# A four-layer model on one core: dilated pieces spread over the expert turns, gathers of sequences 1 to 3 released earlier, and one-hots of the slot table moved from GpSimd to VectorE

## The chip, the cores and the metric

The kernel runs on one core of a Trainium2 chip. The metric is the device time of one execution in microseconds (us). The engines are named as in the profile: PE (TensorE, matrix products and transposes), DVE (VectorE), ACT (ScalarE), POOL (GpSimd, which also issues the indirect transfers) and SP (which issues the direct transfers).

## The reference

Four layers work on x of 4 sequences x 256 tokens x 256 features in f32. Every layer normalises x and adds an attention branch and a feed-forward branch of the same normalised input:

```python
xn = _layernorm(x)
x = x + attention(xn) + feed_forward(xn)     # four layers, each with its own two branches
```

- Layer 0: a gated linear scan, and a gated feed-forward network.
- Layer 1: dilated attention (segments of 64 tokens, 16 heads of 16 features, even heads see the even tokens of a segment, odd heads the odd ones), and 32 experts of which each token takes the 4 best:

```python
logits = x @ gate_w.T + gate_b
topk_logits, topk_idx = jax.lax.top_k(logits, K)            # E = 32, K = 4
topk_weight = softmax(topk_logits)
gate, up = ragged_dot(xt, w_gate, sizes) + b_gate, ragged_dot(xt, w_up, sizes) + b_up
gate, up = minimum(gate, 7), clip(up, -7, 7)
outs = ragged_dot((up + 1) * gate * sigmoid(1.702 * gate), w_down, sizes) + b_down
y = sum(outs * topk_weight)
```

- Layer 2: gated attention with 16 heads and two running states, and a block with latent attention and 8 experts (2 of 7 routed, 1 shared).
- Layer 3: causal attention with one head, and 8 experts of which each token takes 2.

## The kernel before, in words

x stays in the core's memory as 16 tiles of 128 tokens x 256 features. Four tiles are one sequence, called a block (NB = 4). `xn` holds the normalised tiles, `xnT` the same with features on the partitions. Each engine executes its own instructions in order. A scheduler places them in that order from the order in which the Python code issues them, from their dependencies, and from marks: under `self.tc.issue_after(self.mark)` instructions come behind the marked one, here the power that ends the last reciprocal root (`rsqrt`, L424: a scaling on POOL at L427 and a power on POOL at L429).

**Layer 1** (`layer1`, L1050) goes through these stages:

- *Places* (`places1`, L1245). The table `in_slot` says which token stands in which row of which expert's slots. For each of 16 tiles and each of a token's 4 experts m, DVE makes a one-hot `lane` (L1254) and DVE (m = 0) or POOL (m = 1 to 3) a one-hot `token` (L1256); PE multiplies the two (L1260) and adds them up. Both have a ring of 8 buffers. Every second tile one piece of the dilated units 0 and 1 is issued beside them.
- *Dilated units*. A unit is one block and one parity of heads: 8 units of 4 pieces each (`dilated`, L1400). The pieces issue (1) v and the queries q, by 8 steps on ACT (`scalar`) or one on DVE and one on POOL (L1421), (2) scores on PE (L1432) and their exponential on ACT (L1435), (3) pv on PE (L1444) and its copy on ACT, (4) transposes on PE (L1453) and the division and addition on DVE (L1455 to L1464).
- *Turns*. Rows gathered by POOL (L1315) are transposed by PE (L1327), multiplied by the expert's gate and up weights (L1343), combined on DVE (L1358), and multiplied by the down weights (L1364). There are 16 static turns (two blocks of rows each, one for each expert, weights loaded in groups), a number of pair turns (19 with these inputs) and of single turns (7), chosen at run time by a switch (`arms1`). Beside static turns `beside1` (L1174) issues the router's remaining products, one piece a turn; beside pair turns `beside2` (L1227) issues six pieces `eq` (four comparisons on DVE at L1238, each with a product on POOL at L1239, and sums) and the pieces of units 2 to 4, at 18 pieces over all pairs; beside the singles stands unit 5.
- *Collecting* (`collect1`, L1266). For one block POOL gathers 16 times 128 rows of the experts' outputs (L1275), and DVE adds each to x with its weight (`accumulate`, L532). The gathers land in the block's own `xn` and `xnT`, so there are 8 destinations and each is used twice. Block 0 is collected with units 6 and 7 beside it, then normalised (`layer_norm`: statistics at L438 and L439, the root on POOL at L427 and L429, `xn` on DVE at L457).

**Layer 2** (`layer2`, L1483) runs 32 gated units, unit u on block u % 4. A unit's supply (`gated_supply`) makes its projections (`pj`, L1659) from Wk, Ws and Wq, the clipped scores' exponential (eF, L1669 on DVE and L1670 on ACT) and transposes (`turn`, L1690); the unit itself makes scores (`sc`, L1722), values (`pt`, L1737) and the rest; the drain adds its output. `run` interleaves the steps of unit u (m), of the supply of u + 1 (s) and of the drain of u - 1 (d) by an order string written out by hand, and beside them the latent chain of the second branch (its first steps: `rmsq` on ACT at L1976, the root `rms` on POOL, `a` on DVE at L1979). The supply of unit u needs its block normalised, and for blocks 1 to 3 `normed` (L1510) first collects that block:

```python
if b:
    with self.tc.issue_after(self.mark):
        for _ in self.collect1(b):
            pass
    self.layer_norm(b)
```

`latent_tables` (L1909) prepares constants of the latent chain on POOL and DVE, among them the memset of `va` (L1915, L1916).

Of the kernel before, what the change touches and what calls it, by code (L numbers as in the profile page):

```python
# [15 lines left out]
NB = 4  # L16
# [99 lines left out]
class Net:  # L116
# [419 lines left out]
    def layer0(self):  # L536
# [9 lines left out]
        with ExitStack() as ctx:  # L546
# [30 lines left out]
                self.load_group(g)  # L577
            self.moe2, self.moe3 = self.expert_rows("l2", 7, 2), self.expert_rows("l3", 8, 2)
            self.latent_ahead(early)
            self.clear1()  # L580
            c_b, d1_b = cols[:, 0:2], cols[:, 6:14]
            agg_b, _, _, _, _, d2_b, bc_b, gate_b, out_g, out_b = (rows[:, i : i + 1, :] for i in range(10))
# [467 lines left out]
    def layer1(self):  # L1050
        nc, a, moe, r1 = self.nc, self.a, self.moe1, self.r1
        with ExitStack() as ctx:
# [17 lines left out]
            nc.scalar.mul(e.rearrange("p (i j) s n -> p i (j s n)", j=4), zeros(4), 0.0)  # L1070

            units = [(b, p) for b in range(NB) for p in range(2)]
            dilated = lambda u: self.dilated(*units[u], e, v, wa, pd, scalar=u < 2)
            early = [dilated(u) for u in range(2)]
            turns = iter([early[0]] * 3 + [early[1]] * 3)
            for _ in self.places1(wk, po):
# [29 lines left out]
            for pairs in self.arms1(0, [1 + 2 * i for i in range(PAIRS // 2 + 1)]):  # L1106
                line = Line(self)
                at = lambda n: 2 * n if n < STATIC // 2 + pairs else None
                pieces = self.beside1(bd, wa, ptr, pd)
                for n in range(STATIC // 2):  # L1110
                    line.turn(
                        dict(t=2 * n, n=n, parts=[static(2 * n), static(2 * n + 1)], done=static_done), at(n + 2)
                    )
                    if n in (8, 10):
                        self.fetch1(singles_at + n - 8, held[n // 2 - 4])
                    next(pieces, None)
                for _ in pieces:
                    pass

                def pair_done(j):  # L1120
                    if 2 <= j < pairs - 8:
                        self.load_expert(8 + (j - 2) % 8, j + 8)

                pieces = self.beside2([dilated(u) for u in (2, 3, 4)], wa)
                credit = 0.0
                for j in range(pairs):
                    line.turn(dict(t=STATIC + 2 * j, n=j, parts=pair(j), done=pair_done), at(STATIC // 2 + j + 2))
                    credit += 18 / pairs
                    while credit >= 0.999:
                        credit -= 1  # L1130
                        next(pieces, None)
                line.end(pieces)
            for singles in self.arms1(1, list(range(17))):
                line = Line(self)

                def single_done(k):
                    for j in (2 * k + 8, 2 * k + 9):
                        if j < 2 * singles:
                            self.load_expert((2 + j) % 8, 32 + j)

                for j in (6, 7):
                    if j < 2 * singles:
                        self.load_expert((2 + j) % 8, 32 + j)
                pieces = dilated(5)
                for k in range(singles):
                    line.turn(
                        dict(t=singles_at + 2 * k, n=k, parts=[single(2 * k), single(2 * k + 1)], done=single_done),
                        singles_at + 2 * k + 4 if k + 2 < singles else None,
                    )
                    next(pieces, None)  # L1150
                line.end(pieces)
            self.latent_loads()
            pieces = (piece for u in (6, 7) for piece in dilated(u))
            for n, _ in enumerate(self.collect1(0)):
                if n % 2:
                    next(pieces, None)
            for _ in pieces:
                pass
            self.layer_norm(0)
        self.routing.close()  # L1160
        self.stats = self.small
        self.ordered.close()
# [8 lines left out]
        for i in self.tc.Switch(index, len(counts)):  # L1171
            yield counts[i]

    def beside1(self, bd, wa, ptr, pd):  # L1174


        nc, r1 = self.nc, self.r1
# [46 lines left out]
                products(b)  # L1224
                yield

    def beside2(self, chains, wa):  # L1227

        nc, r1 = self.nc, self.r1
        slot, s8, w = r1["slot"], r1["s8"], r1["w"]  # L1230
        eqs = []
        for m in range(6):
            if m > 1:
                nc.vector.tensor_reduce(self.share1[:, :, m - 2], eqs[m - 2], AX.X, ALU.add)
            if m < 4:
                eq = wa.tile([P, 4, P], F32, tag="pvs", name="eq").rearrange("p a b -> p (a b)")
                eqs.append(eq.rearrange("p (i e) -> p i e", e=32))
                nc.vector.tensor_tensor(eqs[m], slot, s8[:, :, m : m + 1].to_broadcast([P, NTILE, 32]), ALU.is_equal)  # L1238
                nc.gpsimd.tensor_tensor(eqs[m], eqs[m], w, ALU.mult)  # L1239
            yield  # L1240
        for chain in chains:
            for _ in chain:
                yield

    def places1(self, wk, pool):  # L1245

# [4 lines left out]
        for i in range(NTILE):  # L1251
            for m in range(4):
                lane = wk.tile([P, P], F16, tag="lane", name="lane", bufs=8)
                nc.vector.tensor_scalar(lane, self.lane16, inside[:, i, m : m + 1], None, ALU.is_equal)  # L1254
                token = wk.tile([P, blocks], F16, tag="token", name="token", bufs=8)
                (nc.gpsimd if m else nc.vector).tensor_scalar(  # L1256
                    token, self.starts16[:, :blocks], first[:, i, m : m + 1], self.less[:, i : i + 1], ALU.is_equal,
                    ALU.mult,
                )
# [223 lines left out]
    def layer2(self):  # L1483
# [8 lines left out]
        with ExitStack() as ctx:  # L1492
# [8 lines left out]
            def supplied(u):  # L1501
# [5 lines left out]
                units[u] = {"b": b, "w": weights[pair]}  # L1507
                return self.gated_supply(units[u])

            def normed(b):  # L1510
                if b:
                    with self.tc.issue_after(self.mark):
                        for _ in self.collect1(b):
                            pass
                    self.layer_norm(b)
                yield
                self.to_features(
                    gp["ps"], self.xn[:, 4 * b : 4 * b + 4, :], self.xnT[:, :, b * T : (b + 1) * T], tag="ps"
                )
# [389 lines left out]
    def latent_tables(self):  # L1909
        nc, lp = self.nc, self.lp  # L1910
        rotk, rotq = lp["rot"]
        _, rk, up, _, _, _, shift_row = lp["w_"]
        sign = lp["sign"]
        for t in (self.w2, self.top2, lp["mt"], lp["va"]):
            nc.gpsimd.memset(t, 0.0)  # L1915
        nc.gpsimd.memset(lp["va"][:, :, :, 16:17], 1.0)  # L1916
        nc.gpsimd.memset(sign, 1.0)
        for j, lo in enumerate(lp["lows"]):

# [5 lines left out]
                out=lo, in_=lo, compare_op=ALU.is_ge, fill=1.0, base=32 * j + 31, pattern=[[0, 1]], channel_multiplier=-1  # L1925
            )
            nc.gpsimd.tensor_tensor(sign, sign, lo, ALU.mult)

        cols = lambda t: t.rearrange("p (h r) -> p h r", r=32)
        for k in range(KD):  # L1930
# [584 lines left out]
```

## Time and profile before

| what | value |
|---|---|
| median of 3 runs (lowest to highest) | 2217.51 us (2215.41 to 2227.51) |
| the profiled execution's own time | 2226.35 us |
| its span, first to last instruction | 2224.6 us |
| mean granted clock of PE in it | 0.917 |
| busy: PE, DVE, ACT, POOL | 88%, 54%, 37%, 30% of the span |
| chain that ended last | PE 57%, DVE 9%, issue 6%, POOL 5%, DMA 3% |

The chain that ended last is followed back from the last instruction, at each step to what released it. Times of single instructions come from the one profiled execution; its zero is the start of the span. In a line of the timeline stand start, busy time, engine, line, operation, output and inputs, count, and in brackets the idle time before it with what ended it. Where the kernel is in it: the places run from 177 to 216 us, static turns from about 227 to 291, pair turns to 371, single turns from 376 to 407, block 0 is collected and normalised until 455, and layer 2 follows.

### The profile page before, as it was taken

The numbers are of one execution on the slowest core, as the hardware profiler recorded it, in microseconds if no ns is written. First come the engines' busy times: TensorE is split into PE (matmuls) and PEld (weight loads), VectorE is DVE, ScalarE is ACT, GpSimd is POOL, SyncE is SP. The second block draws the span as 40 slices with busy tenths as digits, with TensorE's granted clock in tenths as the row PEclk, the third lists the DMA queues.
The fourth block names the chain that finished last, engine by engine and source line by source line (L and its number), as shares of the span: only waits on it lengthen the run. The fifth ranks groups of instructions, "written<-read, shape, count | busy, mean of one in ns | idle before, by whom it ended". The sixth has DMA issues, their size and how long they took to land.

```text
span 2224.6 us, 35391 instructions
## 1 busy us (share of the span) xinstructions
PE 1967.7 (88%) x13015; PEld 1441.2 (65%) x13015; DVE 1192.5 (54%) x3422; ACT 825.1 (37%) x1661; POOL 667.0 (30%) x782
## 2 busy tenths in 40 slices
PE   5754988448999999999999999999999988899995
PEld 2422877335666776666766676656787866678895
DVE  5745565458565655554655656555655564522223
ACT  1243344222433433433433444333345533334321
POOL 6328564464112121121111121111444351022231
PEclk9955999768999999999999999998899999899998
DMA  8312885531000000000000000001433320168697
GB/s 287 131 38 66 256 261 148 165 100 43 5 13 6 8 10 6 8 10 6 6 13 6 8 11 5 27 11 41 135 120 113 98 81 1 42 229 266 214 329 242
DMA packets 149548, 198.19 MB, mean 89 GB/s; under 512 B 16885, under 2 KB 127576, under 8 KB 149208
## 3 DMA queue, kind: packets, MB, share of 16 engines
q1 hardware_dynamic: 135224, 156.40, 21.6%
q0 software_dynamic: 14112, 39.15, 6.0%
q8 instruction: 110, 1.80, 0.3%
q14 instruction: 102, 0.84, 0.1%
HBM read 154.21 MB, written 41.29 MB: 88 GB/s over the span
## 4 chain that ended last, share of the span: by engine, by line
PE 57%; DVE 9%; issue 6%; POOL 5%; DMA 3%; ACT 1%; another core or an unknown queue 1%; SPq 0%; POOLq 0%; DVEq 0%; ACTq 0%
PE pt L1737 8%; PE pj L1659 6%; PE o L1850 4%; PE g L2266 4%; PE kq L2081 3%; PE pov L1801 3%; PE sc L1722 3%; DVE junk L2056 2%; PE o L2279 2%; PE qk L2049 2%; PE pv L2097 2%; DMA r<-l_rows,in_slot 2%; PE st L1710 1%; PE turn L1690 1%; PE pov L1807 1%
## 5 line engine op out<-in xcount | busy, mean ns | idle before, releaser
L2056 DVE CUSTOM_DVE_ANT_0 junk<-qk,hide 128x512 f32<-128x512 f32 (+3 forms) x256 | 124.6, 487 | 41.9 <-PE qk L2049 23.9
L2089 POOL TENSOR_SCALAR_AFFINE_SELECT pr<-pr 128x512 f32<-128x512 f32 x64 | 40.3, 643 | 339.1 <-ACT pr L2086 339.1
L2266 PEld LDWEIGHTS g<-rT,we 128*128 128x128 f32 x1120 | 131.4, 193 | 5.4 <-ACT rT L376 3.0
L2266 PE MATMUL g<-rT,we 128*128 128x128 f32 x1120 | 132.3, 277 | 1.9 <-ACT rT L376 1.9
L343 POOL DMA_INDIRECT r<-l_rows,in_slot x73 | 71.2, 975 | 191.4 <-PE rt L374 105.8
L383 POOL DMA_INDIRECT l_outs<-y,to x73 | 72.5, 993 | 183.6 <-ACT y L382 148.9
L1737 PE MATMUL pt<-Wg,xnT 128*128 128x256 f32 x512 | 125.3, 397 | 2.1 <-DVE both L361 1.0
L1850 PE MATMUL o<-Wo,oT 128*128 128x256 f32 x512 | 121.7, 381 | 0.0
L1737 PE MATMUL pt<-Wv,xnT 128*128 128x256 f32 x512 | 120.1, 386 | 0.0
L1728 DVE TENSOR_TENSOR s<-sc,keep 128x512 f32<-128x512 f32 x128 | 82.5, 683 | 68.1 <-PE sc L1722 68.1
L1672 DVE RECIPROCAL rz<-rz 128x128 f32<-128x128 f32 x128 | 116.8, 933 | 0.4
L1737 PEld LDWEIGHTS pt<-Wg,xnT 128*128 128x128 f32 x512 | 97.9, 197 | 26.6 <-issue 8.5
L355 DVE TENSOR_TENSOR mine<-r,number 128x2 f32<-128x2 f32 x73 | 13.1, 180 | 174.8 <-DMA r<-l_rows,in_slot 174.7
L2086 ACT ACTIVATE pr<-kq 128x512 f32<-128x512 f32 (+1 forms) x192 | 86.2, 530 | 50.1 <-PE kq L2081 49.6
L1737 PEld LDWEIGHTS pt<-Wv,xnT 128*128 128x128 f32 x512 | 94.9, 191 | 15.0 <-issue 0.2
L1315 POOL DMA_INDIRECT r<-l_rows,in_slot x84 | 82.8, 986 | 72.2 <-PE rt L1327 30.5
L1850 PEld LDWEIGHTS o<-Wo,oT 128*128 128x128 f32 x512 | 96.0, 197 | 8.3 <-issue 0.5
L2081 PE MATMUL kq<-q,kT 32*128 32x128 f32 (+3 forms) x512 | 89.3, 497 | 7.4 <-DVE mx L2056 5.9
L1818 DVE TENSOR_TENSOR o<-pov,g 128x512 f32<-128x512 f32 x64 | 41.3, 686 | 77.2 <-ACT sq L1817 77.2
L1740 ACT COPY v<-pt 128x512 f32<-128x512 f32 x64 | 37.5, 586 | 120.4 <-PE pt L1737 119.3
L1823 POOL TENSOR_TENSOR rs<-ms,sm 128x8 f32<-128x8 f32 x32 | 6.5, 204 | 240.3 <-DVE ms L1821 240.2
L2033 POOL TENSOR_TENSOR q<-q 128x512 f32<-128x512 f32 x16 | 20.3, 1269 | 192.2 <-DVE q L2030 192.2
(561 smaller groups left out, 4664.6 us busy)
## 6 DMA issues: line engine op xcount, KB each, us to landing
we<-l_w SPq DMA_DIRECT2D x70, 512.0 KB
we<-l_wo SPq DMA_DIRECT2D x35, 512.0 KB
l_outs<-none SPq DMA_DIRECT2D x1, 11776.0 KB
l_outs<-y SPq DMA_DIRECT2D x42, 256.0 KB
we<-l_r_gate SPq DMA_DIRECT2D x38, 128.0 KB
we<-l_r_up SPq DMA_DIRECT2D x38, 128.0 KB
we<-l_r_down SPq DMA_DIRECT2D x38, 128.0 KB
l_rows<-xn SPq DMA_DIRECT2D x8, 544.0 KB
```

Source lines behind the costliest of these rows:

```text
L343: self.nc.gpsimd.indirect_dma_start(out=r[:, m, :], out_offset=None, in_=moe["rows"][:, :], in_offset=bass.IndirectOffsetOnAxis(ap=moe["in ...
L383: self.no_order(moe["name"] + " back", nc.gpsimd.indirect_dma_start(out=moe["outs"][:, :], out_offset=bass.IndirectOffsetOnAxis(ap=to, axi ...
L1315: nc.gpsimd.indirect_dma_start(out=r[:, i, :], out_offset=None, in_=moe["rows"][:, :], in_offset=bass.IndirectOffsetOnAxis(ap=moe["in_slot ...
L1659: nc.tensor.matmul(ps, w[n][:, k, :], self.xnT[:, k, t["b"] * T : (t["b"] + 1) * T], start=(k == 0), stop=(k == KD - 1))
L1672: inverse = lambda c: nc.vector.reciprocal(rz[:, c * P : (c + 1) * P], rz[:, c * P : (c + 1) * P])
L1728: nc.vector.tensor_tensor(s, ps[hh], keep4, ALU.mult)
L1737: nc.tensor.matmul(ps[:, i, :], self.xnT[:, k, s : s + P], w[n][:, k, :], start=(k == 0), stop=(k == KD - 1))
L1850: nc.tensor.matmul(ps[:, p, :], of_parity(oT[:, h, c * D : (c + 1) * D], p), wo[:, h, :], start=(h == 0), stop=(h == 1),)
L2056: nc.vector.tensor_tensor_reduce(out=junk[:, :m], in0=tiles[j][:, off : off + m], in1=self.hide[:, T - m :], op0=ALU.add, op1=ALU.max, sca ...
L2081: nc.tensor.matmul(tiles[j][:, BLOCK[i] - off : BLOCK[i] - off + T - i * P], kT[r, i * P : (i + 1) * P], qT[r, i * P :], start=True, stop= ...
L2086: nc.scalar.activation(pr[:, j, off : off + m], tiles[j][:, :m], AF.Exp, scale=0.25)
L2266: nc.tensor.matmul(pt[:, m, :], we[:, q, k * T + m * P : k * T + (m + 1) * P], rT[:, k, :], start=(k == 0), stop=(k == KD - 1),)
```

## The change

- In `places1` POOL makes only the token one-hots of m = 3; DVE makes m = 0 to 2.
- `beside2` is joined to `beside1`. The 35 pieces left (router, six eq, units 2 to 5) are issued over the static and the pair turns together, at 35 / (16 + pairs - 1) a turn. No dilated piece is left beside the singles.
- The queries of units 6 and 7 are made by ACT. Their pieces stand at fixed gathers of block 0's collection, unit 7's last piece behind block 0's norm.
- The mark that held the gathers of blocks 1 to 3 behind a norm is gone. The gathers are issued in steps of `run` (two a step in unit 0, alternately two and one in units 1 and 2), and these units have another order string. The supply of the next unit is built when its first step is due.
- The memsets and sign selections of the latent tables move to layer 0 (`latent_signs`); only the two memsets of `va` stay in `latent_tables`.

```diff
@@ layer 0
             self.latent_ahead(early)
+            self.latent_signs()
@@ layer1
-            dilated = lambda u: self.dilated(*units[u], e, v, wa, pd, scalar=u < 2)
+            dilated = lambda u: self.dilated(*units[u], e, v, wa, pd, scalar=u < 2 or u > 5)
...
-                pieces = self.beside1(bd, wa, ptr, pd)
+                pieces = self.beside1(bd, wa, ptr, pd, [dilated(u) for u in (2, 3, 4, 5)])
+                credit, rate = 0.0, 35 / (STATIC // 2 + pairs - 1)
                 for n in range(STATIC // 2):
...
-                    next(pieces, None)
-                for _ in pieces:
-                    pass
+                    credit += rate
+                    while credit >= 0.999:
+                        credit -= 1
+                        next(pieces, None)
...
-                pieces = self.beside2([dilated(u) for u in (2, 3, 4)], wa)
-                credit = 0.0
                 for j in range(pairs):
...
-                    credit += 18 / pairs
+                    credit += rate
...
-                pieces = dilated(5)
                 for k in range(singles):
...
-                    next(pieces, None)
-                line.end(pieces)
+                line.end(iter(()))
             self.latent_loads()
-            pieces = (piece for u in (6, 7) for piece in dilated(u))
+            last = [dilated(u) for u in (6, 7)]
+            next(last[0])
+            turns = {1: 0, 4: 0, 5: 1, 8: 1, 10: 0, 12: 1}
             for n, _ in enumerate(self.collect1(0)):
-                if n % 2:
-                    next(pieces, None)
-            for _ in pieces:
-                pass
+                if n in turns:
+                    next(last[turns[n]])
             self.layer_norm(0)
+            for chain in last:
+                for _ in chain:
+                    pass
@@ places1
-                (nc.gpsimd if m else nc.vector).tensor_scalar(
+                (nc.gpsimd if m == 3 else nc.vector).tensor_scalar(
@@ layer2
+            def supplies(u):
+                yield from supplied(u)
+
             def normed(b):
                 if b:
-                    with self.tc.issue_after(self.mark):
-                        for _ in self.collect1(b):
-                            pass
+                    for _ in collects[b]:
+                        pass
                     self.layer_norm(b)
...
-                supply = supplied(u + 1) if u + 1 < UNITS else iter(())
+                supply = supplies(u + 1) if u + 1 < UNITS else iter(())
+                gathered = collects.get(u + 1, iter(()))
...
-                for what in "mmmmsmsmmdmmsmsdmsd" if u + 1 < UNITS else "mmmmdmmdmmdmmm":
+                order = "mmmmsmsmmdmmsmsdmsd" if u + 1 < UNITS else "mmmmdmmdmmdmmm"
+                for n, what in enumerate("mmmmmmmdmmmsmsmdssds" if u < NB - 1 else order):
                     next(chains[what], None)
+                    for _ in range(2 - (u and n % 2)):
+                        next(gathered, None)
...
+            collects = {b: self.collect1(b) for b in range(1, NB)}
@@ latent_tables, its first lines now latent_signs
-        for t in (self.w2, self.top2, lp["mt"], lp["va"]):
+        for t in (self.w2, self.top2, lp["mt"]):
             nc.gpsimd.memset(t, 0.0)
-        nc.gpsimd.memset(lp["va"][:, :, :, 16:17], 1.0)
...
+    def latent_tables(self):
+        nc.gpsimd.memset(lp["va"], 0.0)
+        nc.gpsimd.memset(lp["va"][:, :, :, 16:17], 1.0)
```

More of the change, by code (lines that the diff above doesn't have):

```diff
@@ L1172, in arms1, with beside1 @@
             yield counts[i]
-    def beside1(self, bd, wa, ptr, pd):
+    def beside1(self, bd, wa, ptr, pd, chains):
         nc, r1 = self.nc, self.r1
@@ L1225, in beside1 @@
                 yield
-    def beside2(self, chains, wa):
-        nc, r1 = self.nc, self.r1
         slot, s8, w = r1["slot"], r1["s8"], r1["w"]
@@ L1241, in beside2 @@
         for chain in chains:
-            for _ in chain:
-                yield
+            yield from chain
     def places1(self, wk, pool):
@@ L1907, in latent_loads, with latent_signs @@
         self.load(ow, a["l2_o_w"].rearrange("(k p) n -> p k n", p=P))
-    def latent_tables(self):
+    def latent_signs(self):
         nc, lp = self.nc, self.lp
-        rotk, rotq = lp["rot"]
-        _, rk, up, _, _, _, shift_row = lp["w_"]
         sign = lp["sign"]
-        for t in (self.w2, self.top2, lp["mt"], lp["va"]):
+        for t in (self.w2, self.top2, lp["mt"]):
             nc.gpsimd.memset(t, 0.0)
-        nc.gpsimd.memset(lp["va"][:, :, :, 16:17], 1.0)
         nc.gpsimd.memset(sign, 1.0)
@@ L1927, in latent_tables @@
             nc.gpsimd.tensor_tensor(sign, sign, lo, ALU.mult)
+    def latent_tables(self):
+        nc, lp = self.nc, self.lp
+        rotk, rotq = lp["rot"]
+        _, rk, up, _, _, _, shift_row = lp["w_"]
+        sign = lp["sign"]
+        nc.gpsimd.memset(lp["va"], 0.0)
+        nc.gpsimd.memset(lp["va"][:, :, :, 16:17], 1.0)
         cols = lambda t: t.rearrange("p (h r) -> p h r", r=32)
```

## The prediction

> **What bounds the kernel now.** First the 40 slices of the page, to find where TensorE (PE) is short of work.
>
> ```profile
> PE   5754988448999999999999999999999988899995
> POOL 6328564464112121121111121111444351022231
> PEclk9955999768999999999999999998899999899998
> ```
>
> A slice is 55.6 us. From slice 10 (556 us) on PE stands at 8 or 9, so work there can only be cut, and the change cuts none. The holes lie before: slice 3 (167 to 222 us) and slices 7 to 9 (389 to 556), with POOL at 5 and 4, 4, 6. A microsecond gained there brings forward the start of the full stretch, and so the end. The chain that ended last agrees: PE 57%, DVE 9%, POOL 5%. Second, the table by stage (us, then busy time of PE, PEld, DVE, ACT, POOL, then clock, DMA share, GB/s):
>
> ```profile
> 170.00:216.00 46.00, 19.69 (x193) 11.83 (x194) 25.87 (x114) 17.01 (x33) 40.62 (x50) 0.54 0.22 70
> ...
> 411.00:455.00 44.00, 10.18 (x137) 7.40 (x137) 16.70 (x45) 6.88 (x15) 23.75 (x23) 0.51 0.35 110
> 455.00:500.00 45.00, 23.50 (x104) 14.92 (x105) 25.38 (x60) 10.67 (x31) 33.81 (x37) 0.65 0.40 120
> 500.00:545.00 45.00, 37.98 (x175) 21.49 (x171) 39.42 (x98) 7.66 (x14) 22.77 (x24) 0.81 0.19 56
> 545.00:700.00 155.00, 153.44 (x1057) 101.73 (x1056) 91.35 (x217) 63.13 (x113) 25.18 (x28) 0.98 0.02 7
> ```
>
> In 170 to 216 POOL is busy 40.62 of 46. Between 411 and 545 PE is idle 62 of 134 us; after 545 it is full. Third, POOL's and PE's timelines in that hole:
>
> ```profile
> 411.83 1.80 POOL L1915 MEMSET both<- 128x2048 f32 x1 [20.30 <-DMA l_outs<-y]
> ...
> 452.96 0.20 POOL L427 TENSOR_SCALAR rs<-mv 128x4 f32<-128x4 f32 x1 [13.78 <-DVE mv L439]
> 453.24 1.05 POOL L429 TENSOR_TENSOR rs<-rs,neghalf 128x4 f32<-128x4 f32 x1
> ...
> 475.35 1.04 POOL L429 TENSOR_TENSOR rms<-rms,neghalf 128x4 f32<-128x4 f32 x1
> ```
>
> ```profile
> 448.27 1.11 PE L1453 MATMUL pvt<-ident,pvs 128*128 128x128 f32 x4 [0.71 <-ACT pvs L1449]
> 454.79 2.08 PE L472 MATMUL tr<-ident,xn 128*128 128x128 f32 x8 [5.41 <-DVE xn L457]
> ...
> 488.76 2.08 PE L472 MATMUL tr<-ident,xn 128*128 128x128 f32 x8 [6.58 <-DVE xn L457]
> 490.77 2.08 PE L1722 MATMUL sc<-qT,kT 64*128 64x128 f32 x16
> ```
>
> Expert outputs are complete at 411.83; block 0 is normalised when unit 7's last piece is through (448.27), and gated unit 0's first scores (490.77) stand on PE behind the features of block 1, whose 16 gathers POOL only starts after block 0's norm.
>
> **Part 1, the places.** Each of 16 tiles needs 4 lanes and 4 tokens. Now POOL makes 48 tokens in one piece of 38.91 us (176.96 to 215.87), 0.81 each:
>
> ```profile
> L1256 POOL TENSOR_SCALAR token<-starts,first,less x48: 786/791/1094, 177.0 to 215.1; 128x126 f16<-128x126 f16 x48
> L1256 DVE TENSOR_SCALAR token<-starts,first,less x16: 299/348/449, 178.3 to 210.2; 128x126 f16<-128x126 f16 x16
> ```
>
> After, POOL makes 16 (16 x 0.81 = 13 us, no longer the limit) and DVE 48. DVE's steps in its timeline: four lanes take 0.81 us (190.20 to 191.01), a token 0.22 to 0.26. A tile is 0.81 + 3 x 0.24 = 1.53, 16 tiles 24.5: from 176.96 to 201.4. PE also carries six pieces of units 0 and 1 here, and its next one-hot product waits behind each: the ring of 8 lanes lets DVE run two tiles (3 us) ahead, while the wait for e on ACT is 1.28 (table) + 2.43 plus scores of 1.9 for unit 0 and 2.43 + 1.9 for unit 1. That leaves 2.6 + 1.4, and 1.3 for the last products and in_slot: 206.7 against 216.2, a gain of 9.5; I take **9.2**. Bounds: DVE tokens at a step of 0.31 add 3.4, so 6; no stall left, 13.
> The rows above were taken with POOL busy beside DVE throughout, so they hold what the two do to each other. The Trainium skill, "GPSIMD Engine Reference", section 1 (Specifications), speaks against the move: GpSimd's SBUF interface is shared with VectorE, and two-port modes contend. By it, DVE one-hots at their slowest (0.45) would make the 48 tokens 10 us longer and the gain nothing; the steps of 0.22 to 0.26 beside a busy POOL do not show that, and I go by them.
> Everything from the first gather (216.82) moves with it: DMA share is 0.43 in 216 to 240 and 0.98 in 240 to 270 with PE busy 29.87 of 30, so loads do not yet hold PE there.
>
> **Part 2, dilated units 2 to 5.** 35 pieces at 35/34 a turn: 16 now fall into the 16 static turns and 19 into the 19 pair turns. Before it was 13, the end, and 18. Unit 5's scores (1.08), pv (1.08) and pvt (0.60) go from the singles to the pairs, where PE is full (40.03 of 41.00 in 330 to 371): +2.8. The singles lose 1.81 + 1.08 + 0.60 = 3.5, partly idle anyway. The eq products on POOL (1.31 each, behind DVE's, with gathers queued behind; PE waits of 0.52, 1.58, 1.09 and 2.12 in 292 to 330) start in static turns instead: the same waits earlier. I take **0**, bounds -4 and +4.
>
> **Part 3, units 6 and 7.** q goes from POOL (2 x 1.9) and DVE (2 x 1.22) to 8 ACT steps of 0.42 a unit. From 411.17: v 0.5, q 3.4, scores 1.9, e 2.4, pv 1.9; unit 7 behind it ends about 437, 11 us before 448.27. It leaves the path.
>
> **Part 4, gathers and norm.** Block 1 to 3's gathers lose the mark that held them behind block 0's norm. In the changed program's POOL order that norm's rs stands behind 39 gathers and two memsets, its power behind 40; before, behind 16. A gather costs 0.96 + 0.30 issue = 1.26. 411.83 + 39 x 1.26 + 2.0 = 463.0; 0.3, one gather, power 1.05: xn starts at 465.6 against 454.32. This is 11.3 **late**: DVE's xn, PE's features and three products wait for it, and PE is idle from 437 to 466.
> What is won comes after. Then 8 gathers (10.1), rms and rs 0.5, one gather 1.26, power 1.05: 478.6 (475.35 + 1.04 before). DVE: three a at 0.38, eF 0.7: 480.4. ACT's exponential 0.7, then rmsq of block 1 and qT (0.6 each): 482.9. Unit 0's scores now stand ahead of block 1's features on PE: **482.8 against 490.77**. The last gather is issued about 505 (528.55 before), so no later unit waits longer for its block than before, and I carry **8.0** through to 545. Bounds: 0 if a chain of unit 0 that was hidden sets the pace, 16 if unit 1's gathers now cost PE nothing. The order strings of units 0 to 2 only permute work in a stretch that waits; SP's latent loads now precede Wk, Ws, Wq, all needed only at 468, 50 us after issue. latent_signs adds about 1 us of POOL work before the start's rs; PE then waits 3.33 us for weights (at 23.66): 0. A latent memset of 1.8 moves behind 22 gathers, counted above.
>
> **Sum.** 9.2 + 0 + 8.0 = 17.2. The profiled execution (2226.35 = span 2224.6 + 1.75 around it) becomes 2209.2, its span 2207.4. It lies 8.8 above the median of 2217.51; the stages moved are far shorter than that ratio could touch, so I take the same 17.2 from the median: **2200.3**.
>
> **Rivals.** (a) *Given back*: the norm that is 11 us late. At a pitch of 1.43 a gather, 49 gathers delay unit 0 by 49 x 0.17 = 8 and part 4 brings nothing; with places at 6 to 9 the time is 2208 to 2212. For it: blocks 1 to 3 took 1.56 a gather before, norms and waits included (454.48 to 529.5). Against: pitch 1.26 wherever POOL did not wait. (b) *Slower*: the same queue at a worse pitch. Eight transfers are in flight, and each gather waits for the one eight before and, in a block's second half, for DVE's accumulation, which stands in order among others. From a pitch of 1.83 unit 0 is 28 - 8 = 20 late, places give back 9, and the time is 2228.6; at 2.0 it is 2237. For it: DVE accumulates of block 0 now stand behind block 1's. Against: landing took about 3 us (454.48 to 457.51), far below eight pitches. (c) *More*: places 13, part 4 16: 2188. (d) *Spread does nothing*: part 4's gathers are not beside gated units at all, since 39 of 64 precede the norm; true of the order, and already in my sum.
>
> **Numbers.** No change is within 0.5%, 11 us: 2206 to 2229. My forecast (2194 to 2206) 0.44, (c) 0.16: faster 0.60. (a) and smaller gains 0.28. (b) 0.12. Range 2186 to 2228: above it lies (b), below it all parts at their best.
>
> **What would show it.** in_slot at about 207 with POOL's tokens no longer one solid block; outputs complete near 402; POOL's rs of block 0 after 39 gathers, 51 us after that; unit 0's scores 71 us after it, not 79; unit 1's (546.24 before) at 529. Wrong if DVE's tokens step by over 0.45, if gathers step by over 1.43, or if PE's idle time between the last expert and the full stretch, now 62 us, is not some 8 smaller.

## The result, and the profile after

The change makes the kernel slightly slower, by less than 1%. Beside runs of the kernel before (median 2221.35 us) the changed kernel has a median of 2235.62 us (2224.51 to 2250.46); the ratio is 1.0073, 95% interval 1.0052 to 1.0095. The forecast was 2200.3. The profiled execution took 2224.51 us, its span is 2222.8 us, and it is the fastest of the changed kernel's runs.

The slices of the changed kernel's page, to be laid beside those of before:

```profile
PE   5755988158999999999999999999999988899995
POOL 6324573553112112121111121111444352022231
PEclk9955999568999999999999999999899999899998
```

Slice 3 of POOL has gone from 8 to 4: the places no longer fill it. The hole of PE has moved forward with layer 1 (slice 7 holds 1, slice 8 holds 5), but it isn't narrower, and slice 9 is still 8. The table by stage says the same in microseconds (length, then busy time of PE, PEld, DVE, ACT, POOL, then clock, DMA share, GB/s):

```profile
170.00:216.00 46.00, 21.55 (x212) 14.14 (x213) 34.42 (x165) 17.05 (x33) 23.59 (x27) 0.57 0.30 92
...
411.00:455.00 44.00, 6.26 (x72) 4.01 (x72) 14.43 (x41) 7.24 (x16) 27.83 (x29) 0.50 0.30 87
455.00:500.00 45.00, 28.86 (x144) 19.36 (x145) 25.20 (x67) 14.16 (x37) 24.23 (x28) 0.73 0.32 96
500.00:545.00 45.00, 36.37 (x154) 19.66 (x153) 35.43 (x88) 7.31 (x13) 18.12 (x18) 0.81 0.09 24
545.00:700.00 155.00, 149.51 (x1002) 96.28 (x1002) 85.91 (x196) 60.18 (x109) 22.41 (x24) 0.98 0.02 7
```

Layer 1 ends 14.9 us earlier (ACT's copy of the last down product is through at 394.3 against 409.2). Between 411 and 545 PE is still idle 62.5 of 134 us, as before, although this stretch now begins 15 us later in the work; and from 545 to 700, which was full, PE is idle 5.5 us. What layer 1 won is lost in the first gated units.

The places themselves, the token rows of the changed kernel:

```profile
L1254 DVE TENSOR_SCALAR token<-starts,first,less x48: 300/308/437, 177.9 to 203.8; 128x126 f16<-128x126 f16 x48
L1254 POOL TENSOR_SCALAR token<-starts,first,less x16: 802/860/893, 176.7 to 202.6; 128x126 f16<-128x126 f16 x16
```

POOL's 16 tokens no longer fill the stretch (16 x 0.86 = 13.8 of 26 us), the chain of lanes and tokens on DVE sets the pace, and `in_slot` is done at 204.9 against 216.5.

### The profile page after: what moved, and what is told of

It is laid out like the page before. It is cut to its first block, busy times and chain, and to the rows that moved or that the text cites. A ratio compares the mean times of both kernels' runs of the same rounds, so it can differ in the third digit from the quotient of the medians.

```text
span 2222.8 us, 35354 instructions
## 1 busy us (share of the span) xinstructions
PE 1959.6 (88%) x13015; PEld 1432.5 (64%) x13015; DVE 1188.3 (53%) x3448; ACT 833.8 (38%) x1681; POOL 641.3 (29%) x748
## 4 chain that ended last, share of the span: by engine, by line
PE 55%; issue 8%; DVE 8%; POOL 6%; DMA 3%; ACT 2%; another core or an unknown queue 1%; SPq 0%; POOLq 0%; DVEq 0%; ACTq 0%
PE pt L1742 8%; PE pj L1664 6%; PE o L1855 4%; PE kq L2091 3%; PE sc L1727 3%; PE pov L1806 2%; PE g L2276 2%; PE qk L2059 2%; DVE junk L2066 2%; PE pv L2107 2%; DMA r<-l_rows,in_slot 2%; POOL l_outs L383 1%; PE turn L1695 1%; PE st L1715 1%
## 5 line engine op out<-in xcount | busy, mean ns | idle before, releaser
L2066 DVE CUSTOM_DVE_ANT_0 junk<-qk,hide 128x512 f32<-128x512 f32 (+3 forms) x256 | 124.1, 485 | 42.8 <-PE qk L2059 24.5
L355 DVE TENSOR_TENSOR mine<-r,number 128x2 f32<-128x2 f32 x73 | 12.8, 175 | 182.0 <-DMA r<-l_rows,in_slot 175.7
L2091 PE MATMUL kq<-q,kT 32*128 32x128 f32 (+3 forms) x512 | 90.3, 485 | 9.7 <-DVE mx L2066 8.1
L2091 PEld LDWEIGHTS kq<-q,kT 32*128 32x128 f32 x512 | 40.0, 189 | 55.8 <-DVE mx L2066 34.4
```

The lines of the kernel that those rows point to most:

```text
L2066: nc.vector.tensor_tensor_reduce(out=junk[:, :m], in0=tiles[j][:, off : off + m], in1=self.hide[:, T - m :], op0=ALU.add, op1=ALU.max, sca ...
L2091: nc.tensor.matmul(tiles[j][:, BLOCK[i] - off : BLOCK[i] - off + T - i * P], kT[r, i * P : (i + 1) * P], qT[r, i * P :], start=True, stop= ...
```

## The experiments

Lines of the changed kernel are a few lower than before's (L1727 is `sc`, L1664 `pj`, L2091 `kq`, L1451 `pvt`). Four chips served the experiments, A to D in the order below, each with its own runs of the kernel before; ratios are against those. One number sorts the profiles better than the span, because it has no part of the 1,550 us that follow: the time from T0, POOL's first instruction after its wait for the experts' outputs, to the scores of units 0 and 4. In the kernel before, v1_places and v3_layer2 that instruction is the memset of the latent tables, 2.2 us ahead of block 0's first gather; in the others it is the gather. The kernel before was profiled on the first chip only.

| kernel | chip | T0 | to unit 0 | to unit 4 | ratio (95%) |
|---|---|---|---|---|---|
| before | first | 411.8 | 78.9 | 255.5 | 1 |
| after | first | 397.7 | 81.4 | 273.1 | 1.0073 (1.0052 to 1.0095) |
| v1_places | A | 397.2 | 79.1 | 254.9 | 0.9938 (0.9918 to 0.9958) |
| v2_layer1 | A | 398.6 | 73.8 | 251.0 | 0.9930 (0.9906 to 0.9955) |
| v3_layer2 | A | 408.7 | 87.1 | 275.8 | 1.0129 (1.0108 to 1.0151) |
| v4_after | A | 397.5 | 81.4 | 272.8 | 1.0051 (1.0026 to 1.0076) |
| v5_order | B | 401.5 | 63.5 | 266.9 | 1.0017 (0.9998 to 1.0036) |
| v6_hoist | B | 399.8 | 72.2 | 247.4 | 0.9944 (0.9926 to 0.9962) |
| v8_spread | B | 402.3 | 72.1 | 247.3 | 0.9957 (0.9938 to 0.9976) |
| v10_hold | B | 398.9 | 65.8 | 243.0 | 0.9931 (0.9910 to 0.9953) |
| v7_drain | C | 396.0 | 71.9 | 246.8 | 0.9957 (0.9940 to 0.9973) |
| v9_half | C | 400.6 | 72.0 | 256.5 | 0.9990 (0.9972 to 1.0009) |
| v12_both | C | 397.5 | 45.3 | 239.4 | 0.9958 (0.9943 to 0.9974) |
| v13_after | C | 401.5 | 71.9 | 260.5 | 1.0011 (0.9991 to 1.0031) |
| v14_marks | D | 399.6 | 43.8 | 234.0 | 0.9889 (0.9871 to 0.9906) |
| v15_hold | D | 397.7 | 65.5 | 243.4 | 0.9937 (0.9911 to 0.9963) |
| v16_hoist | D | 397.6 | 72.3 | 245.2 | 0.9949 (0.9932 to 0.9967) |
| v17_after | D | 396.6 | 72.3 | 260.9 | 1.0015 (0.9995 to 1.0035) |

### Which half loses: chip A

**v1_places** is the kernel before with one line of the change:

```diff
-                (nc.gpsimd if m else nc.vector).tensor_scalar(
+                (nc.gpsimd if m == 3 else nc.vector).tensor_scalar(
```

> The kernel before with the places' edit alone (POOL makes the token one-hots of m = 3 only). Theory A (the layer-1 part gains, the layer-2 part gives it back): in_slot 11 to 12 us earlier, as in the changed kernel (204.9 against 216.5), and all of it at the end: 9 to 12 us under before. Theory B (what is gained ahead of layer 2 is swallowed there whatever layer 2 does): in_slot as early, but the total within 4 us of before.

2208.85 us against 2224.2. **v2_layer1** is the changed kernel with layer 2's steps as before:

```diff
-                    for _ in collects[b]:
-                        pass
+                    with self.tc.issue_after(self.mark):
+                        for _ in self.collect1(b):
+                            pass
...
-                for n, what in enumerate("mmmmmmmdmmmsmsmdssds" if u < NB - 1 else order):
+                for what in "mmmmsmsmmdmmsmsdmsd" if u + 1 < UNITS else "mmmmdmmdmmdmmm":
```

> The changed kernel with layer 2's supplies, mark and order string as before: places, spread, units 6 and 7 and latent_signs are kept. Theory A: block 0's norm stands behind 16 gathers again; its xn starts 12 to 16 us earlier than before's 454.3, and the total is 12 to 16 us under before, some 2206. Theory B: 2221 to 2236, like before or the changed kernel.

2210.21 us. **v3_layer2** is the reverse: the kernel before with those steps of layer 2 as the change has them.

> The kernel before with layer 2's part of the change alone (no mark, gathers in the steps of run, new order string). Theory A: unit 0's scores no earlier than before, unit 4's 15 us later, and the total 15 to 25 us over before, 2236 to 2246. Theory B: within 5 us of before. A third reading C, that the two parts only hurt together (units 6 and 7 among hoisted gathers): also within 5 us of before, but then the run with layer 1 alone is faster.

2255.37 us. **v4_after** is the changed kernel again.

> The changed kernel once more, for a second profile. Its 19 executions lay between 2224.5 and 2250.5, the profiled one at the lowest. Theory A: some 14 us over before on this chip. If the profile falls at 2240 or above, its mean clock is 0.915 instead of 0.925 and the extra half-clock time tells where the spread arises; ACT's wait of 32.8 us before the copy of unit 6's pv shows whether it comes back.

2232.14 us. The directions are theory A's, the sizes are not: v1_places gains 15 us (9 to 12 were expected), v3_layer2 loses 31 (15 to 25), v4_after 8 (14). So the places alone bring 0.6%, the rest of layer 1's part adds nothing that these intervals can see, and layer 2's part loses 1.2 to 1.3% on this chip whichever layer 1 it stands behind: the forecast had it at 8 us of gain.

### The hoist and the order string: chip B

**v5_order** is v2_layer1 with the new order string alone, so the marks that hold the gathers are back:

```diff
-                for what in "mmmmsmsmmdmmsmsdmsd" if u + 1 < UNITS else "mmmmdmmdmmdmmm":
+                for what in "mmmmmmmdmmmsmsmdssds" if u < NB - 1 else order:
```

> The run with layer 1's part alone, plus the new order string of units 0 to 2 (eager supplies and the mark stay). Theory A1 (of the 22 us that layer 2's part costs, the order string costs most: units 0 to 3 took 60.3 + 51.6 + 45.4 us against 57.6 + 45.3 + 39.7, 14.7 us more): total 10 to 15 us over the layer-1 run, near 2222; unit 0's scores as early (472) and unit 4's 10 to 15 us later (660 to 665). Theory A2 (the gathers between cost it): within 3 us of the layer-1 run.

2218.57 us against 2215.46. **v6_hoist** is the changed kernel with the old string alone; its gathers stay released:

```diff
-                for n, what in enumerate("mmmmmmmdmmmsmsmdssds" if u < NB - 1 else order):
+                for n, what in enumerate(order):
```

> The changed kernel with the old order string in units 0 to 2; gathers without the mark and issued in the steps of run as changed. A1: xn of block 0 still at 460, 25 us later than with the mark, unit 0's scores near 479, but units 0 to 2 at the pace of before: total 10 to 15 us under the changed kernel, near 2222. A2: within 3 us of the changed kernel, 2235.

2201.22 us. The string carries the loss: it takes away with the old gathers what layer 1 won (0.993 for v2_layer1 and v10_hold, 1.0017 for v5_order), and leaving it out gives it back with the new ones. With the old gathers it costs more than expected: 20.8 us between v10_hold, described below, and v5_order, which also differ in v10's copy, against 10 to 15 expected. **v8_spread** is v1_places with units 2 to 5 spread over the turns:

> The kernel with the places' edit alone, plus the spread of units 2 to 5 over static and pair turns. Prediction's part 2: 0 (-4 to +4) against the places alone. Rival: the six eq pieces now stall the last static turns (PE idle 6.3 us in 270 to 292 in the changed kernel, none before), 3 to 6 us over the places alone.

2206.45 us, 0.9957 against 0.9938 for v1_places on another chip: so 0.19%, 4 us, slower, with intervals that overlap. That fits the forecast of nothing, and it fits the rival of 3 to 6 us as well. On one chip, v2_layer1, which has the spread too, stands level with v1_places. **v10_hold** is v2_layer1 with a copy on POOL that reads unit 6's products, so that the later gathers of block 0 wait for them:

```diff
-            turns = {1: 0, 4: 0, 5: 1, 8: 1, 10: 0, 12: 1}
+            turns = {1: 0, 7: 0, 8: 1, 10: 0, 11: 1, 13: 1}
...
+        if b == NB - 1 and p == 0:
+            nc.gpsimd.tensor_copy(self.small.tile([P, 4], F32, tag="wsum", name="hold"), pvs[:, 0, :4])
```

> The run with layer 1's part alone, with one copy of 4 columns on POOL that reads unit 6's pv copy and so holds gathers 9 to 16 of block 0 back until it is made; unit 6's pv stands at gather 7. Theory P (PE's last product of a piece is reported late while POOL issues gathers: 406.5 by the record, 421.4 by ACT, POOL's sixteenth gather ending at 418.3): with POOL stopped after 8 gathers the copy starts within 2 us of pv's end, near 408 to 411, the norm of block 0 comes up to 8 us earlier, and the total is 3 to 8 us under the layer-1 run. Rival Q (the delay is PE's or ACT's own, fetching instructions after the switch): the copy starts at 421 again, gathers 9 to 16 wait for it, and the total is 10 us over.

2197.79 us, level with v2_layer1's ratio. It decides nothing between theories P and Q: on this chip the copy follows the recorded end of the product within 0.1 us without the hold as well (v5_order, v6_hoist).

### What in the string: chip C

The new string differs twice (steps counted from 0): the drain of the unit before comes at step 7 instead of 9, and the first steps of the next unit's supply (s) come at 11 instead of 4. **v7_drain** keeps the supply where it was and takes the early drain, **v9_half** puts the first two steps of the supply early and the last three late:

```diff
-                for n, what in enumerate("mmmmmmmdmmmsmsmdssds" if u < NB - 1 else order):
+                for n, what in enumerate("mmmmsmsdmmmmsmsmdmsd" if u < NB - 1 else order):
```

```diff
-                for n, what in enumerate("mmmmmmmdmmmsmsmdssds" if u < NB - 1 else order):
+                for n, what in enumerate("mmmmsmsdmmmmmmmdssds" if u < NB - 1 else order):
```

> The changed kernel with the old order string in units 0 to 2, except that the first drain step stands at place 7 instead of 9, as in the new one (mmmmsmsdmmmmsmsmdmsd). Theory S (the new string costs because the next unit's supply, five steps of projections, exponential and reciprocals, starts at step 11 instead of 4): as fast as with the old string, some 13 us under before (ratio near 0.994). Theory D (the early drain costs): 15 us or more slower than that.

> The changed kernel with the first two supply steps at their old places and the last three late, as in the new string (mmmmsmsdmmmmmmmdssds). Theory S: if the first two steps (kT, the clipped exponential and the sums that the reciprocals need) are what must start early, the time is within 5 us of the old string's; if all five must be spread over the unit, it lies halfway to the changed kernel, 8 to 15 us slower than the old string. Theory D: like the changed kernel.

> The changed kernel on the same chip as the three others. Theory S: 15 to 29 us slower than with the first drain step alone moved. Its third profile tells whether ACT's late start of unit 6's pv copy (32.8 and 33.6 us so far) belongs to this program: then it is there again; if it belongs to the chip or the run, it is gone here, as it was in the two runs on another chip.

Against 2216.32 before: v7_drain 2206.89, v9_half 2215.00, v13_after (the changed kernel once more) 2221.21. The early drain costs nothing. Half of the delay costs 8.1 us, all of it 14.3.

**v12_both** takes v10_hold's layer 1 and the old string, and puts the released gathers of blocks 1 to 3 behind block 0's norm:

```diff
-                    for _ in range(2 - (u and n % 2)):
-                        next(gathered, None)
+                    with self.tc.issue_after(mark):
+                        for _ in range(2 - (u and n % 2)):
+                            next(gathered, None)
...
+            mark = self.mark
```

> Layer 1 as in the run with the held gathers, layer 2 with the old string and the gathers of blocks 1 to 3 issued in the steps of run, but behind block 0's norm. Unit 0's scores then stand ahead of block 1's features on PE and behind only 16 gathers. Theory S: norm at 428, unit 0's scores by 450 (465 with the held gathers, 472 with the hoisted ones), and the total 5 to 15 us under both, a ratio near 0.987. Rival: unit 1 then waits for block 1, whose norm stands behind 49 gathers, and the total is that of the two others, 0.993.

2207.72 us, 0.9958: the 0.987 did not come. Unit 0 begins 27 us sooner after T0 than in v7_drain (45.3 against 71.9), but unit 4 only 7 us sooner: most of it is lost in unit 0, where PE's timeline of v12_both has this line:

```profile
474.92 0.47 PE L472 MATMUL tr<-ident,xn 128*128 128x128 f32 x1 [18.25 <-DVE xn L457]
```

The features of block 1 wait 18.25 us, for block 1's norm stands on POOL behind 49 gathers, those of blocks 2 and 3 among them (`rs` at 471.85), as the rival said.

### One chip for the disputed pair, and a better order: chip D

**v16_hoist** and **v17_after** are v6_hoist and the changed kernel again, on one chip, differing in the string alone. **v15_hold** is v10_hold again. **v14_marks** is v12_both with a mark for each block, so that block b's gathers go behind block b - 1's norm:

```diff
-                    with self.tc.issue_after(mark):
+                    with self.tc.issue_after(marks[b - 1]):
...
                     self.layer_norm(b)
+                    marks[b] = self.mark
...
-                    with self.tc.issue_after(mark):
+                    with self.tc.issue_after(marks.get(u, self.mark)):
```

> The changed kernel with the order string of before in units 0 to 2 (v6_hoist once more), on one chip with the changed kernel. Theory (the string costs some 12 us by supplying the next unit late): 0.994 of before, 10 to 14 us below v17_after. Rival (what made the changed kernel slow on two chips was the late report of dilated unit 6's product, which v6's chip did not have): equal to v17_after where neither shows the late report, and slower with it where both do.

> The changed kernel once more. Theory: 1.001 of before if the copy of dilated unit 6's products follows within 1 us of the last product's recorded end, 1.005 to 1.007 if it stands some 30 us behind it. Rival (the late report belongs to the program): it stands there on this chip too, whatever the time.

Against 2216.58 before: v16_hoist 2203.54, v17_after 2216.29. The string costs 12.8 us by the medians. The granted clock, and so the rest of the span, differs from execution to execution; the stretch of units 0 to 3 alone, by each kernel's own boundaries (units 0, 1, 2, then all four), shows the loss directly. First v16_hoist, then v17_after:

```profile
469.87:520.56 50.69, 44.81 (x243) 28.92 (x242) 44.83 (x111) 12.99 (x30) 18.21 (x20) 0.86 0.12 35
520.56:566.53 45.97, 44.04 (x288) 28.60 (x285) 29.03 (x72) 19.36 (x33) 7.20 (x8) 1.00 0.00 1
566.53:608.23 41.70, 41.70 (x299) 27.19 (x295) 24.13 (x52) 16.01 (x30) 6.54 (x8) 1.00 0.04 10
...
469.87:642.85 172.98, 165.17 (x1097) 109.76 (x1096) 119.38 (x286) 62.10 (x119) 37.75 (x42) 0.96 0.06 16
```

```profile
468.86:526.40 57.54, 48.43 (x238) 28.93 (x237) 48.15 (x117) 14.98 (x32) 23.67 (x24) 0.81 0.10 30
526.40:577.97 51.57, 47.49 (x289) 30.08 (x288) 26.54 (x66) 17.83 (x31) 7.24 (x8) 0.97 0.01 1
577.97:623.34 45.37, 44.57 (x296) 28.11 (x295) 24.04 (x50) 16.51 (x30) 7.35 (x7) 0.96 0.04 10
...
468.86:657.48 188.62, 174.62 (x1096) 111.77 (x1096) 119.29 (x285) 63.64 (x121) 40.27 (x42) 0.92 0.05 15
```

The same work (1097 and 1096 products, DVE busy 119.38 and 119.29) takes 15.6 us longer: 6.9 in unit 0, 5.6 in unit 1, 3.7 in unit 2, and nothing in unit 3 (0.5 less), from which on the strings are equal. PE's idle time grows from 7.8 to 14.0, which is 6.2. The clock falls from 0.96 to 0.92 of full, which is (0.08 x 188.6) - (0.04 x 173.0) = 8 us, give or take 2 for the rounding. Where it comes from is seen in the projections of unit 2, of which PE's rows inside unit 1 give the time (v16_hoist, then v17_after; the middle of the three durations is the median):

```profile
L1664 PE MATMUL pj<-xnT,Wk x4: 592/592/592, 530.5 to 531.8; 128*128 128x512 f32 x4
...
L1664 PE MATMUL pj<-xnT,Ws x4: 592/592/697, 536.9 to 538.3; 128*128 128x512 f32 x4
```

```profile
L1664 PE MATMUL pj<-xnT,Wk x4: 668/920/1057, 554.4 to 556.4; 128*128 128x512 f32 x4
...
L1664 PE MATMUL pj<-xnT,Ws x4: 592/592/697, 561.9 to 563.3; 128*128 128x512 f32 x4
```

With the old string Ws is projected 29.6 us ahead of unit 2's scores (536.9 to 566.53), and the exponential, the scan and four reciprocals on DVE and ACT are through at 550.7, 16 us before the scores. With the new one it is projected 16.1 us ahead (561.9 to 577.97), and the same DVE steps run from 565.0 to 573.3, the last 13 us, in turn with the latent chain's maxima. PE's timeline of v17_after has two waits in unit 1, one ahead of the projection and one behind the crowded DVE:

```profile
554.43 2.99 PE L1664 MATMUL pj<-xnT,Wk 128*128 128x512 f32 x4 [1.82 <-issue]
...
569.13 1.13 PE L2091 MATMUL kq<-q,kT 32*128 32x384 f32 x4 [2.26 <-DVE mx L2066]
```

Together they are all of the unit's idle time (51.57 - 47.49 = 4.08). What ended the first isn't shown ("issue"). Behind it, from 555.2 to 558.6, PE was granted half its clock (0.50), and there the four products with Wk take a median of 920 ns instead of 592.

> The kernel of v10_hold once more, as the measure for v14 on the same chip. Both theories: 0.993 of before (0.991 to 0.995).

> The kernel of v12_both with one mark for each block: the gathers of block b wait for the norm of block b-1 (v12 let all three blocks' gathers go behind block 0's norm, and block 1's norm then stood behind 49 gathers). Theory (a unit's start is set by the gathers ahead of its block's norm on POOL): block 1's norm stands behind 32 gathers of its own and block 2's go after it, unit 0's scores stay at about 45 us after the outputs, PE's idle time of 18 us for block 1's features shrinks to under 8, and the time is some 10 us below v12's ratio: about 0.990 to 0.992 of before. Rival (the full stretch's start is set by the sum of 64 gathers, not by their order): as v15_hold, 0.993, within 0.2 per cent.

v15_hold 2202.30, and v14_marks 2190.50: 1.1% below before (0.9889), the fastest of all. With one mark for each block the hoist does bring something. POOL's and PE's timelines of v14_marks:

```profile
457.69 0.19 POOL L427 TENSOR_SCALAR rs<-mv 128x4 f32<-128x4 f32 x1 [3.58 <-DVE mv L439]
```

```profile
443.47 1.87 PE L1733 MATMUL sc<-qT,kT 64*128 64x128 f32 x16
...
459.96 1.11 PE L472 MATMUL tr<-ident,xn 128*128 128x128 f32 x8
```

Unit 0's scores stand 43.8 us after T0, and block 1's norm follows 14 us later, as soon as its statistics are there; its features no longer wait. Unit 4 is reached 234.0 us after T0, 9.4 sooner than in v15_hold on the same chip and 21.5 sooner than before on the first.

## Why the prediction was wrong

**The step that failed** is in part 4: "The order strings of units 0 to 2 only permute work in a stretch that waits", carried at nothing. The string costs 12.8 us (v16_hoist to v17_after), 14.3 with the drain's place held (v7_drain to v13_after). It is wrong in both halves. The stretch does not wait throughout: of the kernel before's units 0 to 2 only unit 0 lies in the hole (PE idle 7.0 of 55.4 us). These are the rows of units 1 and 2, idle 0.8 us and not at all:

```profile
546.16:593.01 46.85, 46.02 (x283) 30.78 (x282) 25.89 (x66) 19.20 (x34) 7.82 (x10) 0.93 0.00 1
593.01:632.72 39.71, 39.71 (x287) 26.01 (x286) 22.83 (x48) 15.88 (x30) 5.75 (x7) 1.00 0.04 11
```

The prediction's own table had PE full from 545 on. And a permutation isn't free where a supply has a latency of its own: the string moved the projections that feed DVE's and ACT's chain to the end of the unit that was there to cover it. The prediction named no cover for this edit, and so no price for its loss. How the loss splits further is only partly shown: PE's idle time and the clock account for at most 14 of the 15.6 us in this pair (they overlap in part), while v9_half, 9.5 us longer than v7_drain in units 0 to 3, has no more idle time than it (7.4 against 8.5); there it lies in the clock (0.92 against 0.94, some 4 us) and within PE's busy records. The second failed term is the 8.0 of part 4, answered below.

**Part 1** had the right mechanism and sign, and the size 9.2 was low: `in_slot` moves 11.6 us in the changed kernel, and the places alone are worth 0.62%, 14 us (v1_places). The 4.0 us for PE's own pieces came as forecast: DVE, in its steps from 177.9 to 204.1, stands 2.78 and 1.26 us behind PE's products, where 2.6 and 1.4 were worked out:

```profile
191.67 0.25 DVE L1252 TENSOR_SCALAR lane<-lane,inside 128x128 f16<-128x128 f16 x1 [2.78 <-PE in_slot L1258]
201.37 0.26 DVE L1252 TENSOR_SCALAR lane<-lane,inside 128x128 f16<-128x128 f16 x1 [1.26 <-PE in_slot L1258]
```

What was too large is the term for the steps themselves: 22.2 us instead of 24.5. The Trainium skill, "GPSIMD Engine Reference", section 1, says VectorE and GpSimd share an SBUF interface. DVE's median token is 308 ns with POOL busy 23.6 of 46 us, and was 348 beside 40.6: the direction agrees, but no run here separates it from other causes, and the 10 us worked out from DVE's slowest token did not come.

**Part 2**, nothing, holds within the intervals (v8_spread), which do not exclude a loss of some 4 us. **Part 4's gathers** came out to within a microsecond or so, where the condition below did not disturb them. POOL's root and PE's first features and scores in v16_hoist:

```profile
448.86 0.19 POOL L427 TENSOR_SCALAR rs<-mv 128x4 f32<-128x4 f32 x1
```

```profile
451.89 2.08 PE L472 MATMUL tr<-ident,xn 128*128 128x128 f32 x8 [19.65 <-DVE xn L457]
...
469.87 2.08 PE L1727 MATMUL sc<-qT,kT 64*128 64x128 f32 x16
```

T0 is 397.60: `rs` 51.3 after it (51 was said), the scores 72.3 (71.0 was said). But the gain of 8 was taken against the wrong base. **Part 3** said of units 6 and 7 "It leaves the path", and the sum gave that no worth, because the hoisted gathers take its place there. With the gathers still held, the other edits bring unit 0's scores forward by themselves: 72.1 us after T0 with the spread (v8_spread), 63.5 to 65.8 with ACT's queries too (v5_order, v10_hold, v15_hold), against 79 in the kernel before on the first chip, of which some 4.5 are the late report told below. (Unit 7's last transposes end 35 us after T0 in v17_after, not the 25 that were worked out, but block 0's norm does not wait for them.) So the hoist as made gives up 6 to 9 us there, wins it back by unit 4 (245.2 to 247.4 against 243.0 to 243.4, nearly), and nets nothing: 0.9944 and 0.9949 with it, 0.9930 to 0.9937 without. The runs without it also build each supply ahead, and v10_hold and v15_hold have their copy, so the nothing belongs to these edits together.

**The rivals.** Rival (b), slower by a gather pitch over 1.83, had the sign and not the cause: the gathers kept 1.25 us, and in v16_hoist and v17_after the norm came when it was forecast. One wait that it named, a gather's for DVE's accumulation, does come where the delay below is. Rival (a)'s pitch of 1.43 did not come either; what it says of 49 gathers ahead of a unit held in another place: v12_both has its 49 gathers ahead of a norm, block 1's, and loses 18 us there.

**Slips in the working.** The steps behind 480.4 add up to 482.3, not 482.9. POOL's digits in slices 3 and 7 to 9 are 8 and 4, 6, 4, not 5 and 4, 4, 6. Unit 1's scores before stand at 546.16. None of these moves the forecast by more than 1 us.

**On two chips there was more.** In the profiles of the changed kernel on the first chip and on A, the scores of unit 0 stand 81.4 after T0, not 72. Its timelines, ACT's, PE's and POOL's:

```profile
437.09 0.59 ACT L1447 COPY pvs<-pv 128x512 f32<-128x512 f32 x1 [32.78 <-remote]
```

```profile
404.36 1.93 PE L1442 MATMUL pv<-e,v 128*32 128x128 f32 x32 [3.18 <-issue]
439.78 1.08 PE L1430 MATMUL sc<-q,xnT 128*32 128x128 f32 x16 [33.48 <-issue]
```

```profile
446.38 0.95 POOL L1273 DMA_INDIRECT xnT<-l_outs,at  x1 [8.89 <-DVE x L532]
```

Dilated unit 6's product ends at 406.3 by its record, ACT's copy starts 31 us later and PE's next piece 33 (a late report, for short). DVE's accumulations stand in order behind that unit's division, and POOL's 31st gather waits 8.89 us for one. So the norm behind it is late, and block 0's features follow T0 by 63.4 us, not 54.3: 9 us. On C and D the copy follows the product's recorded end within 0.1 us, and there the changed kernel is at 1.0011 and 1.0015.

The kernel before has a late report on the first chip too, at unit 6's scores, which end at 426.46 by their record:

```profile
429.83 2.42 ACT L1435 ACTIVATE e<-sc 32x512 f32<-32x512 f32 x4 [18.16 <-remote]
```

Here it is 3.4 us, and 4.5 with the copy that follows 1.2 late. The difference between the two kernels is then some 4.5 us, an estimate: 1.0015 becomes 1.0035, against 1.0051 (1.0026 to 1.0076) and 1.0073 (1.0052 to 1.0095) measured where the report is late. So it explains part of the difference between the chips; the rest is open, and only the profiles show the delay, not the timed runs. The string, on top of a hoist that nets nothing, turned the forecast gain into no change; on two chips something more, of which the late report is at most a part, made it a loss.

## What to carry to other kernels

Before pricing a reordering at nothing, list what each moved step feeds and where its consumer stands: a step that starts a chain over other engines needs the distance that the old order gave it, even beside an engine that looks idle on average. Price a prefetch against the kernel with the change's other parts in, not against the kernel before, since two parts may shorten the same wait. And release transfers no further than the next norm that has to pass them on the same queue: one mark for each block turned a hoist that netted nothing into a gain of 12 us (v15_hold to v14_marks, the same layer 1 on one chip).

## What the runs showed of the hardware

- The late report needs the chip or its condition, whatever the program; its length differs with the program. On the first chip and on A all six profiles have a wait in dilated unit 6 that ends with "remote": ACT's `e` starts 3.4 and 3.7 us behind the recorded end of the scores (before, v1_places), its `pvs` 10.5 to 31.6 us behind that of the product (v3_layer2, v2_layer1, the changed kernel twice). None of the twelve profiles on B, C and D has one, with the changed kernel itself among them. Its cause is open.
- The granted clock differs between profiled executions in stretches that the edits do not touch: from 700 to 1500 us PE was granted 0.96 in v12_both and 0.98 in v14_marks, 16 us give or take 8 for the rounding. That is as much as any part of this change, so spans of single executions do not decide between such kernels.
- A unit can lose clock without idle records: unit 2 of v17_after is idle 0.8 us and is granted 0.96. The Trainium skill, "TensorE: Matmul & The Clock Gate", Part 1, ties the lower clock to an idle window of some 3.4 us; the records here show no such hole in that unit.
